# A gated delta rule whose GpSimd and VectorE instructions issue in the order in which they are written

## The chip, the cores and the metric

One core of one Trainium2 chip. The metric is the device time of one execution in microseconds (us), lower is better. A profile of one execution gives the engines' instructions: PE (TensorE), with PEld for its weight loads, DVE (VectorE), ACT (ScalarE), POOL (GpSimd) and SP (SyncE, which here only issues DMAs). L12 is line 12 of the kernel.

## The reference, cut to what matters

A decoder layer over 4 sequences of 512 tokens and 512 channels: a gated delta rule with 16 heads of 128, a cross attention with fake quantisation, and an attention with a mixture of 8 experts. Each of the three takes a layer norm of x, and adds its result to x. Only the first is changed:

```
q = conv_silu(x @ Wq.T)          # causal, four taps; the same for k and v
g = exp(-exp(A_log) * softplus(x @ Wa.T + dt_bias)); beta = sigmoid(x @ Wb.T)
q, k = l2norm(q), l2norm(k)
def step(S, (q_t, k_t, v_t, g_t, beta_t)):
    error = v_t - g_t * (S.T @ k_t)
    S = g_t * S + outer(k_t, beta_t * error)
    return S, S.T @ q_t
o = o * rsqrt(mean(o*o) + eps) * norm_w * silu(x @ Wg.T)
return o @ Wo.T
```

## The kernel before

The delta rule is computed in chunks of 128 tokens, four to a sequence (`TB`). Within a chunk the recurrence is a triangular system: a strictly lower matrix `at`, made of k @ k.T with its decays, has to be inverted as (1 - A). After that a chunk takes a few matmuls with the state.

The work goes by pairs of heads (`HG` = 2): 4 sequences of 8 pairs, 32 pairs (`NP`), numbered m. The work of a pair is cut into Python generators, each of which emits instructions and yields between them:

- `stage1(m)`: key and query projections and convolutions (`conv`: four matmuls L503, one ACT L511, three DVE instructions L514, a Silu L517), transposes of the keys, the norms `ss` and what follows from them on POOL (`rk`, `ee`, `ke`, `nr`, L558 to L562), the decays `em` by a scan on DVE (L567) and scaled on ACT (L397), the matrix `at` (L579), written to DRAM (`at_d`), the scaled query `qg` (L590), `pt` (L601) and the query norms `rq`. `load_blocks` brings the 32x32 blocks of `at` of all chunks into `iA`, one block to a partition, and an identity into `iT`.
- `stage2_inverse(m)`: inverts those blocks by elimination, 31 steps of two instructions (L644, L645), on DVE for even m and on POOL for odd m. It writes `iT` to DRAM (`t_d`, L648), copies its transpose over `iA` (L649), writes that (`x_d`, L650), and loads both back as whole chunks, `T` (L653) and `X` (L655).
- `stage2_values(m)`: value projection, convolution and transposes (`vn`, L674), and the gates `gs`.
- `stage3(m)`: four joins, which make the inverse of 128x128 from the blocks (matmuls L704/L705, L714/L716, L727, L736, with copies from PSUM between them, L707 to L738), then the chunks in turn: `r` (DVE L760), `u` (ACT L769), the state (DVE L782), the output in `po` (PE L785, L787). The gates are multiplied by the query norms on POOL (L745) before the first chunk. At the end `og` (L796) and `cv` (L800) read `po`, a Square on ACT (L802, L804) and a sum on POOL (`acc`, L805) follow.
- `output(m)`: og @ Wo added up in `xa` over the pairs of a sequence (L825, L830); after a sequence's last pair the normalised result is added to x, which is loaded again into `x_in` (L821), and written to `x1d` (L843, L845).
- `prologue(b)` makes the layer norm, its transpose and the gates of a sequence, `prepare` the keys and values of the cross attention.

The main loop runs `stage3(m)` and, after each of its 15 yields, one turn of everything else; what is left is run at the end of the pair. In a turn `stage1` and `stage2_inverse` take two steps, the others one:

```
            if m:
                rest.append((output(m - 1), 1))
            if m + 2 < NP:
                ...
                rest.append((stage1(m + 2), 2))
            if m + 1 < NP:
                rest.append((stage2_values(m + 1), 1))
                rest.append((stage2_inverse(m + 1), 2))
            ...
            rest = turns(*rest)
            for _ in stage3(m):
                next(rest, None)
            run(rest)
```

So the elimination of pair m + 1 is written beside `stage3(m)`, and the matrix that it needs was written beside `stage3(m - 1)`. That is the order of writing. The framework then schedules: it orders each engine's instructions by its own estimate of when each can start, with the written order as priority, and sets semaphores for every dependence. Each engine works through its queue in the order so fixed. A tile with `bufs=n` has n buffers, used in turn; an allocation waits until the readers of the buffer's last contents are done.

Of the kernel before, what the change touches and what calls it, by code (L numbers as in the profile page):

```python
# [98 lines left out]
def decoder(ctx: ExitStack, tc: tile.TileContext, a: dict, out: bass.AP):  # L99
# [69 lines left out]
    def idle(n):  # L169
        for _ in range(n):  # L170
            yield
# [154 lines left out]
    with ExitStack() as st:  # L326
# [74 lines left out]
        def prologue(b):  # L401

            x = []
            for c in range(TB):
                t = w2.tile([P, D], F32, name="x_in", bufs=4)
                nc.sync.dma_start(t, x_t[:, b * TB + c, :])
                x.append(t)
            yield
            yield
            for c, t in enumerate(x):  # L410
                run(layernorm(t.unsqueeze(1), t.unsqueeze(1), small))
                if c == 0:
                    xnT = s2.tile([P, KD, S], F32, name="xnT", bufs=2)
                    seqs[b] = [xnT]
                tp = p_b.tile([P, KD, P], F32, name="pb")
                for kd in range(KD):
                    nc.tensor.transpose(tp[:, kd, :], t[:, kd * P : (kd + 1) * P], ident)
                nc.scalar.copy(xnT[:, :, c * P : (c + 1) * P], tp)
                yield
            pab = p_b.tile([P, TB, 32], F32, name="pb")  # L420
            for c in range(TB):
                for kd in range(KD):
                    nc.tensor.matmul(pab[:, c, :], xnT[:, kd, c * P : (c + 1) * P], wab[:, kd, :], start=kd == 0, stop=kd == KD - 1)
            g_a, lg, beta, gam, ngam, gend, gall = (seq.tile([P, H1, TB], F32, name=n) for n in ("g_a", "lg", "beta", "gam", "ngam", "gend", "gall"))
            nc.scalar.activation(beta, pab[:, :, 16:32].rearrange("p i h -> p h i"), AF.Sigmoid)
            nc.vector.tensor_tensor(g_a, pab[:, :, 0:16].rearrange("p i h -> p h i"), along(dtb, TB), ALU.add)


            y, z, w = (small.tile([P, H1, TB], F32, name=n, bufs=1) for n in ("sp_y", "sp_z", "sp_w"))
            nc.vector.scalar_tensor_tensor(y, g_a, -1.0, g_a, ALU.mult, ALU.min)  # L430
            nc.scalar.activation(y, y, AF.Exp)
            yield
            nc.vector.tensor_scalar(w, y, 2.0, None, ALU.add)
            nc.vector.reciprocal(w, w)
            nc.vector.tensor_tensor(z, y, w, ALU.mult)
            nc.vector.tensor_tensor(w, z, z, ALU.mult)
            nc.vector.tensor_scalar(y, w, 1.0 / 17, None, ALU.mult)
            for n in (15, 13, 11, 9, 7, 5, 3):
                nc.vector.scalar_tensor_tensor(y, y, 1.0 / n, w, ALU.add, ALU.mult)
                if n in (11, 5):  # L440
                    yield
            nc.vector.scalar_tensor_tensor(y, y, 1.0, z, ALU.add, ALU.mult)
            nc.vector.tensor_scalar(y, y, 2.0, None, ALU.mult)
            nc.vector.scalar_tensor_tensor(y, g_a, 0.0, y, ALU.max, ALU.add)
            nc.vector.scalar_tensor_tensor(y, y, -1.0, along(alog, TB), ALU.mult, ALU.mult)

            nc.vector.tensor_scalar(lg, y, -200.0, None, ALU.max)
            yield

            lgf = lg.rearrange("p h i -> p (h i)")  # L450
            pg = p_b.tile([P, 3, H1 * TB], F32, name="pb")
            for n, m in enumerate((C_UP, C_LO, C_ONE)):
                nc.tensor.matmul(pg[:, n, :], tab_a[:, m, :], lgf, start=True, stop=True)
            for n, dst in enumerate((gam, gend, gall)):
                nc.scalar.activation(dst.rearrange("p h i -> p (h i)"), pg[:, n, :], AF.Exp)
            nc.vector.tensor_scalar(ngam, gam, -1.0, None, ALU.mult)
            yield

            nc.vector.tensor_scalar(y, lg, -87.0, None, ALU.max)
            nc.vector.tensor_scalar(z, y, float(np.log2(np.e)), None, ALU.mult)  # L460
            nc.vector.tensor_scalar(z, z, MAGIC, MAGIC, ALU.add, ALU.subtract)
            nc.vector.scalar_tensor_tensor(y, z, -0.693145751953125, y, ALU.mult, ALU.add)
            nc.vector.scalar_tensor_tensor(y, z, -1.42860677e-06, y, ALU.mult, ALU.add)
            yield
            nc.vector.tensor_scalar(w, y, 1.0 / 5040, None, ALU.mult)
            for n in (720, 120, 24, 6, 2, 1):
                nc.vector.scalar_tensor_tensor(w, w, 1.0 / n, y, ALU.add, ALU.mult)
            n2 = small.tile([P, H1, TB], mybir.dt.int32, name="n2", bufs=1)
            nc.vector.tensor_scalar(n2, z, 127.0, None, ALU.add)
            nc.vector.tensor_scalar(n2, n2, 23, None, ALU.logical_shift_left)  # L470
            nc.vector.scalar_tensor_tensor(w, w, 1.0, n2.bitcast(F32), ALU.add, ALU.mult)
            yield

            tp = p_b.tile([H1 * TB, 2, P], F32, name="pb")
            nc.tensor.transpose(tp[:, 0, :], w.rearrange("p h i -> p (h i)"), ident)
            nc.tensor.transpose(tp[:, 1, :], gam.rearrange("p h i -> p (h i)"), ident)
            gr = w2.tile([P, TB * 64], F32, name="Y6").rearrange("p (n t) -> p n t", n=2)[0 : H1 * TB]
            nc.scalar.copy(gr, tp)
            nc.gpsimd.memset(gr[:, 0, 0:1], 0.0)
            for n in range(2):  # L480
                nc.sync.dma_start(g_d[b, n], gr[:, n, :])
            seqs[b] += [beta, gam, ngam, gend, gall]
            yield
# [38 lines left out]
        def stage1(m):  # L522
# [48 lines left out]
            for p in range(HG):  # L571
                scale(em[p], em[p], ee, p)
                pk = p_b.tile([P, TB, P], F32, name="pb")
                for c in range(TB):
                    k_ = kT[p][:, c * P : (c + 1) * P]
                    nc.tensor.matmul(pk[:, c, :], k_, k_, start=True, stop=True)
                at = live.tile([P, TB, P], F32, name="at", bufs=6)
                ats.append(at)
                nc.vector.scalar_tensor_tensor(at, pk, -1.0, em[p], ALU.mult, ALU.mult)  # L579
                nc.sync.dma_start(squares(at_d[m % SLOTS][p * TB : (p + 1) * TB]), at)  # L580
# [5 lines left out]
            for p in range(HG):  # L586
                q = s1.tile([P, S], F32, name="qh")
                yield from conv(b, hg, p, 0, wq, q)
                g = live.tile([P, S], F32, name="qg", bufs=4)
                nc.gpsimd.tensor_tensor(g, q, mb[p], ALU.mult)  # L590
                qg.append(g)
                t = w2.tile([P, S], F32, name="cv", bufs=5)
# [4 lines left out]
                for c in range(TB):  # L597
                    cs = slice(c * P, (c + 1) * P)
                    nc.tensor.matmul(pq[:, c, :], kT[p][:, cs], q[:, cs], start=True, stop=True)
                t = live.tile([P, TB, P], F32, name="pt", bufs=4)  # L600
                nc.vector.tensor_tensor(t, pq, em[p], ALU.mult)  # L601
                pt.append(t)
                yield
# [86 lines left out]
        def stage3(m):  # L690
# [13 lines left out]
                    nc.tensor.matmul(py[lo[p], c, :], ats[p][:, c, 32:64], Ts[p][:, c, 0:32], start=True, stop=True)  # L704
                    nc.tensor.matmul(py[hi[p], c, :], ats[p][:, c, 96:128], Ts[p][:, c, 64:96], start=True, stop=True)  # L705
            for p in range(HG):
                nc.vector.tensor_copy(Yd[p][32:64, :, 0:32], py[lo[p]])  # L707
                nc.scalar.copy(Yd[p][96:128, :, 32:64], py[hi[p]])
            yield
            px = p_b.tile([P, TB, 96], F32, name="pb")  # L710
# [4 lines left out]
                for p in range(HG):  # L715
                    nc.tensor.matmul(px[half[p], c, 0:64], Yd[p][:, c, :], odd(Xs[p][:, c, :]), start=True, stop=True)  # L716
            for p in range(HG):
                nc.vector.tensor_copy(Ts[p][32:64, :, 0:32], px[lo[p], :, 64:96])
                nc.scalar.copy(Xs[p][0:32, :, 32:64], px[lo[p], :, 0:32])
                nc.vector.tensor_copy(Xs[p][64:96, :, 96:128], px[hi[p], :, 32:64])  # L720
            yield

            Y6 = []
# [17 lines left out]
            t = w2.tile([P, HG, S], F32, name="rrow", bufs=1)  # L741
            nc.sync.dma_start(chunks(t), r_d[m % SLOTS].rearrange("c t -> (c t)").partition_broadcast(P))
            rb = [t[:, p, :] for p in range(HG)]
            for p in range(HG):
                nc.gpsimd.tensor_tensor(gs[p], gs[p], rb[p], ALU.mult)  # L745

            st_ = [None] * HG
            po = [p_o.tile([P, TB, P], F32, name=f"po{p}") for p in range(HG)]
            for c in range(TB):
# [34 lines left out]
                for p in range(HG):  # L784
                    nc.tensor.matmul(po[p][:, c, :], us[p], pt[p][:, c, :], start=True, stop=c == 0)  # L785
                    if c > 0:
                        nc.tensor.matmul(po[p][:, c, :], st_[p], qg[p][:, cs], start=False, stop=True)  # L787
                st_ = nst
                yield

            og = []
# [18 lines left out]
        def output(m):  # L810
# [4 lines left out]
            wot = w2.tile([P, HG, D], F32, name="wot", bufs=2)  # L815
            nc.sync.dma_start(wot, a["a_wo"][hg])
            xs = []
            if hg == NHG - 1:
                for c in range(TB):
                    xs.append(w2.tile([P, D], F32, name="x_in", bufs=4))  # L820
                    nc.sync.dma_start(xs[c], x_t[:, b * TB + c, :])  # L821
            for c in range(TB):
                pw = p_b.tile([P, D], F32, name="pb")
                for p in range(HG):
# [7 lines left out]
            if hg == NHG - 1:  # L832
# [6 lines left out]
                rsqrt(rs, pq, small, add=1e-6, mul=1.0 / VD)  # L839
                yield  # L840
                for c in range(TB):
                    xr = xs[c]
                    nc.vector.scalar_tensor_tensor(xr, xa[c], rs[:, c : c + 1], xr, ALU.mult, ALU.add)  # L843

                    (nc.gpsimd if m == NP - 1 else nc.sync).dma_start(x1d[b * TB + c], xr)  # L845
                    yield

        def prepare():

            ctx_ = [w2.tile([P, D], F32, name="og", bufs=2) for _ in range(2)]  # L850
            for kt in range(2):
                nc.sync.dma_start(ctx_[kt], a["ctx"][kt * P : (kt + 1) * P])
            wk = [w2.tile([P, D], F32, name="x_in", bufs=4) for _ in range(KD)]
            for kd in range(KD):
                nc.sync.dma_start(wk[kd], a["b_wkv"][kd * P : (kd + 1) * P, 0:D])
            wv = [w2.tile([P, HG, D], F32, name="wot", bufs=2) for _ in range(2)]
# [31 lines left out]
            for c in range(KD):  # L888
# [14 lines left out]
                yield  # L903
                nc.sync.dma_start(x_val_d[:, :, c * P : (c + 1) * P], t.rearrange("p (k c) -> p k c", k=2))

        NP = B * NHG
        load_weights(0, 1, 0, 2, 3, by=nc.scalar)
        start = prologue(0)
# [11 lines left out]
        for m in range(NP):  # L920
# [13 lines left out]
                wx = top.enter_context(tc.tile_pool(name="b_x", bufs=2, side="right", reuse_waits="tile"))  # L934
                rest.append((cross(0), 2))
            if m:
                rest.append((output(m - 1), 1))
            if m + 2 < NP:
                if (m + 2) % NHG == 0:
                    assert (m + 2) // NHG in seqs  # L940
# [574 lines left out]
```

## Time and profile before

| | |
|---|---|
| time, median of 3 runs | 3922.55 us (3909.57 to 3927.0) |
| the profiled execution | 3921.34 us, its span 3919.6 us |
| granted TensorE clock, mean | 0.941 |
| busy in the span | PE 3487.2 us (89%), DVE 2238.4 (57%), ACT 1522.5 (39%), POOL 1373.3 (35%) |
| delta rule | about 0 to 2200 us |
| elimination, 16 pairs each | DVE 178.4 + 177.4 us, POOL 249.3 + 275.1 us |

The busy times are sums over instructions; a busy PE need not be at its peak, as matmuls overlap. Which wait ends last at a place is read from the list of waits and the timeline.

### The profile page before, as it was taken

What the parts mean: (1) busy time and instruction counts of PE and PEld (TensorE: products, weight loads), DVE (VectorE), ACT (ScalarE), POOL (GpSimd) and SP (SyncE); (2) the same over time, 40 slices, a digit from 0 to 9 for tenths busy, and PEclk for the clock granted to TensorE, in tenths of its full rate; (3) what the DMA queues carried; (4) which work ended last, traced back from release to release, by engine and by line L of the source; (5) the groups of instructions that cost most, each with busy time, mean ns of one, the idle gap of its engine ahead of it and who ended that gap; (6) DMA issues with size and microseconds to landing.
All of it is one profiled execution on the core that took longest, in us unless ns stands there. A gap on an engine that the chain in (4) does not pass through costs nothing. (4 is left out here: it accounts for less than half of the span.)

```text
span 3919.6 us, 48951 instructions
## 1 busy us (share of the span) xinstructions
PE 3487.2 (89%) x16466; PEld 1984.1 (51%) x16466; DVE 2238.4 (57%) x5115; ACT 1522.5 (39%) x4190; POOL 1373.3 (35%) x1941
## 2 busy tenths in 40 slices
PE   5898899898989989898989799998998999897897
PEld 3455555555555555555555445554554555453343
DVE  5576657675766666756765466555665655543111
ACT  3434443334343434334333244443443444433121
POOL 1443554344435552455335222112212211210442
PEclk8899999899999998999999899998999999898898
DMA  5324332433243333343332444445444444445344
GB/s 163 107 77 123 98 103 80 130 101 111 82 119 119 98 100 106 97 119 104 96 98 87 158 145 154 137 132 132 146 127 137 153 146 139 141 152 183 79 82 93
DMA packets 391881, 465.56 MB, mean 119 GB/s; under 512 B 128451, under 2 KB 242115, under 8 KB 391440
## 3 DMA queue, kind: packets, MB, share of 16 engines
q1 hardware_dynamic: 380080, 438.03, 37.1%
q0 software_dynamic: 10112, 21.58, 3.1%
q8 instruction: 132, 2.16, 0.2%
q10 hardware_dynamic: 1440, 2.84, 0.2%
q14 instruction: 117, 0.96, 0.1%
HBM read 401.76 MB, written 64.81 MB: 119 GB/s over the span
## 5 line engine op out<-in xcount | busy, mean ns | idle before, releaser
L503 PE MATMUL pb<-xnT,w 128*128 128x512 f32 x2048 | 954.9, 605 | 0.0
L503 PEld LDWEIGHTS pb<-xnT,w 128*128 128x128 f32 x2048 | 381.9, 195 | 423.7 <-issue 419.7
L514 DVE SCALAR_TENSOR_TENSOR cv<-pb,pp,cv 128x511 f32<-128x511 f32 (+2 forms) x576 | 427.3, 742 | 153.0 <-ACT cv L511 144.2
L1067 PE MATMUL pb<-c_q,hT 128*128 128x512 f32 x768 | 362.9, 609 | 7.9 <-DMA c_q<-in_c_wq_dram 3.6
L644 POOL TENSOR_TENSOR iW<-iA,iT 32x31 f32<-32x31 f32 (+15 forms) x496 | 249.3, 503 | 210.3 <-DMA iA<-at_d 140.5
L825 PE MATMUL pb<-wot,og 128*128 128x512 f32 x512 | 264.9, 642 | 32.8 <-DVE og L796 26.5
L645 POOL TENSOR_TENSOR iT<-iT,iW 32x31 f32<-32x31 f32 (+15 forms) x496 | 275.1, 555 | 39.0
L1173 PE MATMUL pw<-c_o,oT 128*128 128x512 f32 x512 | 244.8, 611 | 21.9 <-DMA c_o<-in_c_wo_dram 15.5
L511 ACT ACTIVATE cv<-pb,pp 128x512 f32<-128x512 f32 x192 | 148.2, 772 | 261.2 <-PE pb L503 260.7
L1067 PEld LDWEIGHTS pb<-c_q,hT 128*128 128x128 f32 x768 | 143.8, 196 | 162.2 <-issue 149.4
L1139 ACT ACTIVATE e<-pb,nm,rq 128x128 f32<-128x128 f32 (+3 forms) x256 | 158.0, 626 | 104.2 <-DVE nm L1137 75.2
L274 POOL TENSOR_SCALAR x_e<-x_e 128x1024 f32<-128x1024 f32 x64 | 68.7, 1073 | 334.0 <-ACT x_e L269 256.6
L644 DVE TENSOR_TENSOR iW<-iA,iT 32x31 f32<-32x31 f32 (+15 forms) x496 | 178.4, 360 | 11.7 <-DMA iA<-at_d 0.2
L645 DVE TENSOR_TENSOR iT<-iT,iW 32x31 f32<-32x31 f32 (+15 forms) x496 | 177.4, 358 | 11.9
L269 ACT ACTIVATE x_e<-pb,nm 128x256 f32<-128x256 f32 x256 | 118.1, 475 | 164.2 <-DVE nm L266 160.7
L1163 PE MATMUL po<-eT,val 128*128 128x512 f32 x320 | 171.6, 630 | 10.0 <-ACT eT L1161 7.7
L1133 PE MATMUL pb<-kT,qT 128*128 128x256 f32 (+3 forms) x576 | 163.5, 410 | 3.6 <-ACT x_e L269 3.6
L558 POOL TENSOR_TENSOR rk<-ss,mhalf 128x8 f32<-128x8 f32 x32 | 53.1, 1659 | 322.0 <-DVE ss L557 321.9
L579 DVE SCALAR_TENSOR_TENSOR at<-pb,em 128x512 f32<-128x512 f32 x64 | 44.3, 692 | 199.9 <-ACT em L397 199.9
L1173 PEld LDWEIGHTS pw<-c_o,oT 128*128 128x128 f32 x512 | 94.4, 194 | 125.5 <-issue 92.1
L1420 PE MATMUL pb<-w_gu,eT 128*128 x312 | 142.7, 601 | 3.8 <-issue 3.8
L825 PEld LDWEIGHTS pb<-wot,og 128*128 128x128 f32 x512 | 89.7, 194 | 110.3 <-issue 53.3
(324 smaller groups left out, 6609.7 us busy)
## 6 DMA issues: line engine op xcount, KB each, us to landing
c_o<-in_c_wo_dram SPq DMA_DIRECT2D x128, 512.0 KB, 4.1
c_q<-in_c_wq_dram SPq DMA_DIRECT2D x128, 512.0 KB, 4.6
w<-in_a_w_dram SPq DMA_DIRECT2D x124, 512.0 KB, 3.7
row<-g_d SPq DMA_DIRECT2D x64, 512.0 KB, 3.8
at_d<-at SPq DMA_DIRECT2D x64, 256.0 KB, 4.2
T<-t_d SPq DMA_DIRECT2D x32, 512.0 KB, 6.1
X<-x_d SPq DMA_DIRECT2D x32, 512.0 KB, 6.1
rrow<-r_d SPq DMA_DIRECT2D x32, 512.0 KB, 4.7
```

Source lines behind the costliest of these rows:

```text
L503: nc.tensor.matmul(pj, wt[:, kd, p * P : (p + 1) * P], xnT[:, kd, :], start=kd == 0, stop=kd == KD - 1)
L511: nc.scalar.activation(ac, pj, AF.Identity, bias=cb[:, m, h : h + 1], scale=cw[:, m, h, 3:4])
L514: nc.vector.scalar_tensor_tensor(ac[:, j:], pj[:, : S - j], cw[:, m, h, 3 - j : 4 - j], ac[:, j:], ALU.mult, ALU.add)
L644: eng.tensor_tensor(u, A[:, i, i + 1 :].unsqueeze(2).to_broadcast([nb, n, w]), T[:, i, :w].unsqueeze(1).to_broadcast([nb, n, w]), ALU.mult)
L645: eng.tensor_tensor(T[:, i + 1 :, :w], T[:, i + 1 :, :w], u, ALU.add)
L825: nc.tensor.matmul(pw, og[p][:, c * P : (c + 1) * P], wot[:, p, :], start=p == 0, stop=p == HG - 1)
L1067: nc.tensor.matmul(pj, hT[:, kd, :], w[:, kd % 2, :], start=kd == 0, stop=kd == KD - 1)
L1133: nc.tensor.matmul(ps[:, m, k * P : (k + w) * P], qT[g][:, n + m, :], kT[:, g, j : j + w, :], start=True, stop=True)
L1139: nc.scalar.activation(e[n + m][:, :nk], ps[:, m, :nk], AF.Exp, bias=nm[:, n + m : n + m + 1], scale=rq, accum_out=es[:, n + m : n + m + 1])
L1163: nc.tensor.matmul(po, val[:, g, :], eT, start=k == 0, stop=k == c)
L1173: nc.tensor.matmul(pw, oT[:, h + m, :], w[:, m, :], start=g == 0 and h + m == 0, stop=g == 3 and h + m == 3)
L1420: nc.tensor.matmul(pg, hT[:, kd, :], w_gu[:, bass.ds(e, 1), kd, :, :], start=kd == 0, stop=kd == KD - 1)
```

## The change

Within the delta rule, `tc.manual_schedule` is entered for POOL and DVE: the instructions of these two engines keep the order in which they are written. PE, ACT and SP are scheduled as before. With it come edits of buffers and places: `at` has four buffers for six, `qg` and `pt` six for four, `x_in` two for four (so the loads of x are made one at a time, and the final sum goes into `xa`), `prepare` takes `qg` and `pt` buffers for a weight; three copies of the joins go from DVE to ACT; the two products of the gates on POOL are written behind the second and third chunk of `stage3`; and `output` begins one turn later.

```diff
@@ prologue: loads of x
-            for c in range(TB):
-                t = w2.tile([P, D], F32, name="x_in", bufs=4)
+            def load(c):
+
+                t = w2.tile([P, D], F32, name="xa", bufs=4) if b == 0 and c > 1 else w2.tile([P, D], F32, name="x_in", bufs=2)
                 nc.sync.dma_start(t, x_t[:, b * TB + c, :])
                 x.append(t)
...
+            for c in range(TB if b == 0 else 2):
+                load(c)
...
+                if b > 0 and c + 2 < TB:
+                    load(c + 2)
@@ stage1
-                at = live.tile([P, TB, P], F32, name="at", bufs=6)
+                at = live.tile([P, TB, P], F32, name="at", bufs=4)
...
-                g = live.tile([P, S], F32, name="qg", bufs=4)
+                g = live.tile([P, S], F32, name="qg", bufs=6)
...
-                t = live.tile([P, TB, P], F32, name="pt", bufs=4)
+                t = live.tile([P, TB, P], F32, name="pt", bufs=6)
@@ stage3
-                nc.vector.tensor_copy(Yd[p][32:64, :, 0:32], py[lo[p]])
+                nc.scalar.copy(Yd[p][32:64, :, 0:32], py[lo[p]])
...
-                nc.vector.tensor_copy(Ts[p][32:64, :, 0:32], px[lo[p], :, 64:96])
+                nc.scalar.copy(Ts[p][32:64, :, 0:32], px[lo[p], :, 64:96])
                 nc.scalar.copy(Xs[p][0:32, :, 32:64], px[lo[p], :, 0:32])
-                nc.vector.tensor_copy(Xs[p][64:96, :, 96:128], px[hi[p], :, 32:64])
+                nc.scalar.copy(Xs[p][64:96, :, 96:128], px[hi[p], :, 32:64])
...
-            for p in range(HG):
-                nc.gpsimd.tensor_tensor(gs[p], gs[p], rb[p], ALU.mult)
...
+                if 0 < c <= HG:
+                    nc.gpsimd.tensor_tensor(gs[c - 1], gs[c - 1], rb[c - 1], ALU.mult)
                 yield
@@ output
+            def load(c):
+                xs.append(w2.tile([P, D], F32, name="x_in", bufs=2))
+                nc.sync.dma_start(xs[c], x_t[:, b * TB + c, :])
+
             if hg == NHG - 1:
-                for c in range(TB):
-                    xs.append(w2.tile([P, D], F32, name="x_in", bufs=4))
-                    nc.sync.dma_start(xs[c], x_t[:, b * TB + c, :])
+                load(0)
+                load(1)
...
-                    xr = xs[c]
-                    nc.vector.scalar_tensor_tensor(xr, xa[c], rs[:, c : c + 1], xr, ALU.mult, ALU.add)
+                    xr = xa[c]
+                    nc.vector.scalar_tensor_tensor(xr, xr, rs[:, c : c + 1], xs[c], ALU.mult, ALU.add)
+                    if c + 2 < TB:
+                        load(c + 2)
@@ prepare
-            wk = [w2.tile([P, D], F32, name="x_in", bufs=4) for _ in range(KD)]
+            wk = [live.tile([P, S], F32, name="qg", bufs=6) for _ in range(2)]
+            wk += [chunks(live.tile([P, TB, P], F32, name="pt", bufs=6)) for _ in range(2)]
@@ main loop
+        st.enter_context(tc.manual_schedule(engines={mybir.EngineType.Pool, mybir.EngineType.DVE}))
         NP = B * NHG
...
             if m:
-                rest.append((output(m - 1), 1))
+                rest.append((chain(idle(1), output(m - 1)), 1))
```

Behind the edits the numbers of lines are six to twelve higher: L704 becomes L712, L727 L735, L769 L775, L796 L804, L825 L837.

More of the change, by code (lines that the diff above doesn't have):

```diff
@@ L403, in prologue @@
             x = []
-            for c in range(TB):
-                t = w2.tile([P, D], F32, name="x_in", bufs=4)
+            def load(c):
+                t = w2.tile([P, D], F32, name="xa", bufs=4) if b == 0 and c > 1 else w2.tile([P, D], F32, name="x_in", bufs=2)
                 nc.sync.dma_start(t, x_t[:, b * TB + c, :])
                 x.append(t)
+            for c in range(TB if b == 0 else 2):
+                load(c)
             yield
             yield
-            for c, t in enumerate(x):
+            for c in range(TB):
+                t = x[c]
                 run(layernorm(t.unsqueeze(1), t.unsqueeze(1), small))
```

## The prediction

> **What bounds the kernel now.** I read the busy table by stretch first, to see which part the edit can touch and which engine fills it. The columns are stretch, length, then busy us and instruction count of PE, PEld, DVE, ACT and POOL, then granted clock and DMA.
>
> ```profile
> 190.00:2078.00 1888.00, 1702.11 (x8886) 1011.48 (x8886) 1238.31 (x2587) 761.03 (x2125) 867.19 (x1299) 0.94 0.35 102
> 2220.00:3650.00 1430.00, 1301.54 (x5635) 713.51 (x5636) 781.90 (x2048) 593.96 (x1638) 287.73 (x392) 0.96 0.47 146
> ```
>
> The delta rule ends near 2200 us; the rest is untouched. In its 30 steady pairs of heads PE works 1702 of 1888 us, 90%. A pair takes 62.8 us (32 starts of L796 `og`, 210.96 to 2158.74), about 56 of it matmul. So PE sets the rate and what counts is what stops PE. The list of waits, cut to the first 2220 us, PE rows:
>
> ```profile
> PE ps L777 <- ACT u L769: 45.0, 13, 6.0
> PE ps L767 <- DVE r L760: 36.8, 41, 1.5
> PE pb L825 <- DVE og L796: 26.5, 27, 1.0
> PE pb L727 <- DVE cv L514: 22.2, 14, 2.3
> PE ps L758 <- DVE state L782: 20.0, 12, 8.7
> ```
>
> Total us, times, longest. Adding up all holes of the PE timeline from the first join (148 us) to the last (2113 us) gives some 196 us, or 6.3 a pair: all that a better order could win. No row names L704, the first matmul of a pair's joins. Its operand is the inverse, and the timelines of POOL, SP and PE show why it never waits:
>
> ```profile
> 944.42 0.24 POOL L645 TENSOR_TENSOR iT<-iT,iW 32x31 f32<-32x31 f32 x1
> 944.70 0.33 SPq L648 DMA_DIRECT2D t_d<-iT  x1
> 948.56 0.37 SPq L653 DMA_DIRECT2D T<-t_d  x1
> 993.58 0.27 PE L475 MATMUL pb<-tab,sp_w 128*64 128x128 f32 x1
> 993.89 0.22 PE L704 MATMUL pb<-T,at 128*32 128x32 f32 x1
> ```
>
> The elimination of this pair ended at 944.66, its T was fetched at 948.56, and the join came 45 us later. Over all pairs but the last T is issued 20 to 46 us ahead of its join: the scheduler starts an elimination as soon as its `iA` is in, half a pair or more early. That slack is what I follow through the change.
>
> **What the Trainium skill says.** "DVE: scalar operands, raw-bit mode, write accounting and state across instructions", Flops that outlive an instruction: the DVE's queue is one in-order queue. The trace agrees: DVE sits 9.36 us ahead of `at` (L579, 955.87 us) and runs nothing behind it. "DMA: Bandwidth & Descriptors", Anatomy of one DMA: about 2.0 us fixed per transfer, whatever its size; here the 128 KB t_d takes 2.3. "TensorE: Matmul & The Clock Gate", The HAM clock gate: after an idle window of about 3.4 us the array runs at half rate until it has been busy for another. The trace agrees: eight L503 matmuls take 3.60 us at 891.64, but 5.02 at 963.14, soon after a hole of 5.71 us.
>
> **The change part by part.** The built order shows what the new guard does. In the kernel before, the 62 elimination instructions of a pair stand on DVE or POOL well ahead; in the changed one they stand as written, four to each of the 15 turns of `stage3`. Two and the `iA` copy are left for the sixteenth turn, which is emitted after `stage3` has ended. On DVE (even pairs) the queue reads twelve elimination instructions, og x2, cv x2, two, iA. On POOL (odd pairs): rq x2, eight, acc x2, two, iA. SP follows with t_d, x_d, T, iT, X. PE's order is nearly that of before: the last `po` of a pair, at once the first join of the next (all 31), and six convolution matmuls only behind it. So a loop closes that was open before: last po, og, end of elimination, t_d, T, join. Its price, durations from the trace:
>
> Even pair. After the last `r` twelve instructions stand ahead of og, 3.2 us, against some 2.8 of PE until po is done: 0.4. Semaphore 0.15, og x2 1.40, cv x2 1.27, last two 0.17 + 0.19, SP's reaction 0.1, t_d 2.3, reaction 0.2, T 6.1 (median of 32):
>
> ```profile
> L653 SPq DMA_DIRECT2D T<-t_d x32: 370/392/2188, 105.1 to 2108.8; - x32
> DMA to landing us min/median/max: 3.9/6.1/7.1
> ```
>
> That is 12.3 us of idle PE. With no delay ahead of og and the 3.9 us landing it is 9.3; with 7.1, 13.3.
>
> Odd pair. acc needs og 1.40, the first cv 0.68 and ACT's Square 0.63, which is po + 2.8. But POOL's queue first has to get through rq: sr copied (L610), issue and 1.8 us landing, 0.24 + 1.67, then eight eliminations at about 0.4. That is sr + 7.5, with po ending near sr + 3, so po + 4.5; I take this. acc x2 2.61, last two 0.54, reaction 0.1, 2.3, 0.2, 6.1: 16.3 us. From 12.0 (acc at 2.8, T 3.9, t_d 2.2) to 18.
>
> At the same place the kernel before loses 1.0 (`og` to L825). There are 15 even boundaries (pairs 2 to 30) and 16 odd: 15 x 11.3 + 16 x 15.3 = **+414 us**; bounds 300 and 460. X lands about 2 us after T and is read behind six matmuls: no more.
>
> Joins' copies (L707, L718, L720): 192 of 0.29 us go from DVE to ACT, which is busy 761 of 1888 us. This takes L727's waits on DVE, 22.2 + 4.3 us: **-26**. It costs ACT 6 x 0.26 = 1.5 us a pair, hidden behind the six matmuls. Five copies in a row on ACT could also show: 0 to +30, I take 0.
>
> gs products to c = 1, 2 and qg, pt at six buffers: rk on POOL no longer stands behind gs (2.5 us), and pt no longer waits for po (94.2 us of DVE). With that em comes earlier and `u` (45.0 us of PE) less late. But em's two scans, 3.1 us, now stand behind ss. I take half: **-22**, from 0 to -45.
>
> Other waits in order: r and state share DVE with four eliminations a turn (1.4 us), and DVE stays below PE (48.8 of 60 us in an even stretch). The rsqrt round trips over POOL (0.55 us) block DVE. **+15**, from -70 (the r, state and kT waits gone) to +60.
>
> Clock: each stall is over 3.4 us, so PE restarts at half rate. One window costs 1.7 us of work, two 3.4; but PE is at half rate 6% of the time already, partly here. **+31** (1.0 a pair), from 0 to +105.
>
> `at` at four buffers costs nothing: the slot's last reader (L727) is done 20 us before it is written. x_in at two buffers makes the loads of x (L406, L821) serial, 3.5 us each beside turns of 4 us; prologues are hidden, the last output is not, and start and tail run in order too: **+10**, from -10 to +30. `idle(1)` moves `output` a turn later; the stall covers it. `prepare` only takes other buffers: 0. SP carries the same number of transfers.
>
> Sum: 414 - 26 - 22 + 15 + 31 + 10 = **+422**. On the profiled execution (span 3919.6, time 3921.3) that is 4343; the median of the runs shown is 1.2 us higher. PE has room to absorb a little more of so large a hole (the other engines are level when it restarts), so I say 4330.
>
> **The rivals.** *The loop is shorter and better absorbed.* T lands near 4 us as the queues are empty at the boundary, acc starts at po + 2.8, and most of the 170 us of PE's other holes close while everybody catches up: 300 - 120 + 10, about 4110. For it: T and X often landed beside rrow and row before. Against: T and X still run together, and the remaining holes come from the chain r, u, state, which no stall shortens.
>
> *Faster.* If T were in SBUF when the last po ends, the edits would be what is left: L727 26, `u` 45, `og` 26, so 3921 - 97 = 3824. It decides at the join: the elimination would have to end 9 to 12 us before the po of the pair ahead. The built order forbids it, since its last two instructions stand behind og or acc, which read that very po.
>
> *Head-of-line blocking on DVE.* It would have to turn each of about 15 turns of an even pair into a wait of half a us and up: 15 x 0.5 x 15 = 110 us more, 4440. Against: DVE has 11 us free in such a pair and 32 in an odd one.
>
> *The guard does nothing*, the scheduler's order being the written one: 3921 less the 26 for the copies, which measures as no change or a little less. The built orders differ from pair to pair, so this is all but excluded.
>
> **How the numbers follow.** Main case 0.78, shorter loop 0.11, blocking 0.07, faster 0.03, guard void 0.01. The main case's bounds (about 4200 to 4440) with part of the second make 4180 to 4440. A measurement tells some 0.5%, 20 us, from no change; the main case, the shorter loop and the blocking are all slower by far more, so slower 0.96, same 0.01, faster 0.03.
>
> **What would show it.** Right: in the waits of PE a row for L712 on the DMA of T, with 31 waits and 350 to 480 us; a pair at 72 to 78 us, odd boundaries longer by some 4 us; the gap from T's issue to its join down to its landing. L735's wait on DVE gone. Wrong: no such row, or PE holes at the joins below 9 us; then the elimination ends earlier than its place in the queue says. If the row is there and the time is not, the holes elsewhere closed.

## The result and the profile after

The changed kernel takes **4403.1 us** (median of 4 runs, 4395.2 to 4408.8); the kernel before, on the same chip, 3918.4 (3909.6 to 3927.0). The ratio is 1.1228, 95% interval 1.1197 to 1.1259: 485 us slower. The profiled execution has a span of 4407.0 us against 3919.6, 487 us more. The forecast was 4330 with a range of 4180 to 4440.

The same first view as before, busy time by stretch, for 30 pairs of the changed kernel. Columns: stretch, length, busy us and count of PE, PEld, DVE, ACT, POOL, granted clock, DMA share, GB/s.

```profile
190.00:2540.00 2350.00, 1725.30 (x8990) 990.45 (x8989) 1221.34 (x2446) 810.74 (x2321) 917.26 (x1352) 0.87 0.30 85
```

PE works 1725 us, as before, but in 2350 us: 73%, where it was 90%. No other engine is busier. So the time is in holes of PE. The stretch from the first join to the last shows it best, as it holds the same matmuls in every version. The rows are the kernel before, the changed kernel without its guard (an experiment below, in which all other edits are kept), and the changed kernel; columns as above:

```profile
148.53:2113.07 1964.54, 1766.42 (x9278) 1049.82 (x9277) 1270.73 (x2650) 787.81 (x2202) 924.41 (x1388) 0.94 0.36 104
148.23:2097.99 1949.76, 1715.84 (x9277) 1012.52 (x9276) 1228.00 (x2472) 827.75 (x2388) 919.17 (x1389) 0.94 0.36 104
163.55:2576.25 2412.70, 1773.62 (x9278) 1019.85 (x9277) 1244.26 (x2485) 833.32 (x2388) 955.95 (x1417) 0.88 0.29 84
```

Length less PE's busy time is the holes: 198 us before, 234 without the guard, 639 in the changed kernel. The joins come every 77.8 us instead of 63.4. Of the 487 us, 448 lie between those joins (441 of holes, 7 of longer matmuls), 15 ahead of the first and 24 behind the last.

The list of PE's waits (total us, times, longest) up to 2750 us, past the end of the delta rule:

```profile
PE pb L712 <- DMA T<-t_d: 440.6, 31, 17.7
PE pb L607 <- ACT qh L525: 97.0, 52, 11.6
PE ps L764 <- DVE state L788: 42.9, 15, 3.0
PE pb L423 <- DVE x_in L137: 42.3, 14, 6.1
PE ps L773 <- DVE r L766: 19.2, 23, 3.3
```

Before, no row named the join. Now it leads the list with 31 waits, one at every boundary between pairs. The rows that led before are gone or small: L735 (then L727) on DVE is absent, `u` is down from 45.0 us to 0.9, `r` from 36.8 to 19.2. Three others have grown: `qh` from 10.9, `state` from 20.0, the prologue's transposes from 9.7.

An even boundary (into pair 18) in the timeline; the pair ahead has its last `po` done at 1571.53. Columns: start, length, engine, line, instruction, and in brackets the idle time before it:

```profile
1571.76 1.39 DVE L804 SCALAR_TENSOR_TENSOR og<-po,pp,gs 128x512 f32<-128x512 f32 x2
1573.08 1.27 DVE L808 TENSOR_TENSOR cv<-po,rrow 128x512 f32<-128x512 f32 x2
1574.37 0.32 SPq L750 DMA_DIRECT2D rrow<-r_d  x1
1574.47 0.18 DVE L653 TENSOR_TENSOR iT<-iT,iW 32x31 f32<-32x31 f32 x1
1574.81 0.35 SPq L656 DMA_DIRECT2D t_d<-iT  x1
1580.18 0.38 SPq L661 DMA_DIRECT2D T<-t_d  x1
1584.21 0.26 PE L712 MATMUL pb<-T,at 128*32 128x32 f32 x1 [12.68 <-DMA T<-t_d]
```

This is the loop: og, cv, the last elimination step behind them, t_d, T, join. It has nearly the predicted length (12.7 against 12.3 us) but not the predicted parts. t_d takes 5.4 us from issue to T's issue, not 2.5, and T then lands in 4.0, not 6.1:

```profile
L661 SPq DMA_DIRECT2D T<-t_d x32: 376/436/558, 123.9 to 2572.0; - x32
DMA to landing us min/median/max: 4.0/4.2/4.9
```

The next boundary, an odd one (into pair 19), POOL's timeline; `po` ends at 1642.3 and the join comes at 1659.5:

```profile
1643.51 0.24 POOL L630 TENSOR_SCALAR rq<-rq 128x8 f32<-128x8 f32 x1
1643.83 1.67 POOL L631 TENSOR_TENSOR rq<-rq,mhalf 128x8 f32<-128x8 f32 x1
...
1649.05 2.60 POOL L813 TENSOR_TENSOR acc<-acc,cv 128x512 f32<-128x512 f32 x2
...
1652.03 0.24 POOL L653 TENSOR_TENSOR iT<-iT,iW 32x31 f32<-32x31 f32 x1
```

rq, eight elimination instructions, acc, the last two: acc starts 6.8 us after `po` here. The stall is 16 to 17.7 us at most odd boundaries (12.3 to 14.1 at five: the first, the last, and those beside which a prologue has been written). In all the 15 even stalls take 190 us and the 16 odd ones 250.

### The profile page after: what moved, and what is told of

It is laid out like the page before. It is cut to its first block, busy times and chain, and to the rows that moved or that the text cites. A ratio compares the mean times of both kernels' runs of the same rounds, so it can differ in the third digit from the quotient of the medians.

```text
span 4407.0 us, 48821 instructions
## 1 busy us (share of the span) xinstructions
PE 3508.8 (80%) x16466; PEld 1962.6 (45%) x16466; DVE 2202.8 (50%) x4923; ACT 1567.3 (36%) x4379; POOL 1387.0 (31%) x1941
## 5 line engine op out<-in xcount | busy, mean ns | idle before, releaser
L511 PE MATMUL pb<-xnT,w 128*128 128x512 f32 x2048 | 1038.6, 645 | 5.5 <-DVE xa L842 4.0
L511 PEld LDWEIGHTS pb<-xnT,w 128*128 128x128 f32 x2048 | 402.7, 210 | 433.1 <-issue 398.3
L522 DVE SCALAR_TENSOR_TENSOR cv<-pb,pp,cv 128x510 f32<-128x510 f32 (+2 forms) x576 | 423.5, 744 | 67.0 <-ACT cv L519 56.3
L842 DVE TENSOR_TENSOR xa<-pb,xa 128x512 f32<-128x512 f32 x112 | 77.1, 689 | 665.9 <-PE pb L837 665.9
L712 PE MATMUL pb<-T,at 128*32 128x32 f32 x512 | 20.6, 242 | 440.6 <-DMA T<-t_d 440.6
L566 POOL TENSOR_TENSOR rk<-ss,mhalf 128x8 f32<-128x8 f32 x32 | 94.8, 2964 | 805.8 <-DVE ss L565 805.8
L653 POOL TENSOR_TENSOR iT<-iT,iW 32x31 f32<-32x31 f32 (+15 forms) x496 | 264.8, 534 | 38.9
L837 PE MATMUL pb<-wot,og 128*128 128x512 f32 x512 | 257.7, 627 | 1.7 <-issue 1.5
L652 POOL TENSOR_TENSOR iW<-iA,iT 32x31 f32<-32x31 f32 (+15 forms) x496 | 238.3, 480 | 38.9
L712 PEld LDWEIGHTS pb<-T,at 128*32 128x32 f32 x512 | 16.4, 152 | 447.1 <-DMA T<-t_d 406.8
L598 POOL TENSOR_TENSOR qg<-qh,row 128x512 f32<-128x512 f32 x64 | 81.9, 1280 | 387.5 <-ACT qh L525 387.5
L653 DVE TENSOR_TENSOR iT<-iT,iW 32x31 f32<-32x31 f32 (+15 forms) x496 | 186.6, 376 | 17.1
L607 PE MATMUL pb<-qh,kT 128*128 128x128 f32 x512 | 93.3, 338 | 97.0 <-ACT qh L525 97.0
```

The source lines that it names most:

```text
L511: nc.tensor.matmul(pj, wt[:, kd, p * P : (p + 1) * P], xnT[:, kd, :], start=kd == 0, stop=kd == KD - 1)
L522: nc.vector.scalar_tensor_tensor(ac[:, j:], pj[:, : S - j], cw[:, m, h, 3 - j : 4 - j], ac[:, j:], ALU.mult, ALU.add)
L566: nc.gpsimd.tensor_tensor(rk, ss, mhalf[:, 0 : HG * TB], ALU.pow)
L652: eng.tensor_tensor(u, A[:, i, i + 1 :].unsqueeze(2).to_broadcast([nb, n, w]), T[:, i, :w].unsqueeze(1).to_broadcast([nb, n, w]), ALU.mult)
L653: eng.tensor_tensor(T[:, i + 1 :, :w], T[:, i + 1 :, :w], u, ALU.add)
L837: nc.tensor.matmul(pw, og[p][:, c * P : (c + 1) * P], wot[:, p, :], start=p == 0, stop=p == HG - 1)
```

## The experiments

Two theories were on trial. **The loop**: what the written order puts ahead of the elimination's last steps, plus the way through DRAM, makes the stall, and the rest of the loss is other in-order waits. **The buffers**: the other edits (four `at`, two `x_in`, copies on ACT) or the busier queues carry a good part of it. Ratios are to the kernel before on the same chip (medians 3926, 3915 and 3915 us in three groups of runs).

**Without the guard.** All other edits kept.

```diff
-        st.enter_context(tc.manual_schedule(engines={mybir.EngineType.Pool, mybir.EngineType.DVE}))
```

> The changed kernel without the written order: both engines are scheduled, all other edits stay (buffers, joins' copies on ScalarE, gate products behind the chunks, output a turn later). Loop theory: no row of L712; waits of L727/L735 on DVE (26 us), of L825/L837 on og (26) and part of those for u (45) gone: 3830 to 3900. Rival (the edits, not the order, made it slow): above 4200.

3921.3 us, ratio 0.999 (0.9981 to 1.0). No wait at L712. The whole loss needs the guard. The expected gain did not come either. L735 waits 4.7 us (26.5 before) and L837 9.8 (26.5 on og before), but `u` waits 77.4 us (45.0 before) and the prologue's transposes 58.3 us behind `xa`: between the joins the holes grow by 36 us. Against that the same matmuls cover 51 us less, 1716 instead of 1766; why they do isn't shown. The edits by themselves are worth next to nothing, but they move time between matmuls and holes, so what the guard costs has to be read against this kernel.

**Three turns of the elimination to a turn of `stage3`.** Written at this rate, its last step is written some four turns before `stage3` ends.

```diff
-                rest.append((stage2_inverse(m + 1), 2))
+                rest.append((stage2_inverse(m + 1), 3))
```

> The changed kernel with one number altered: a turn takes three steps of the elimination, not two, so its 62 instructions, the iA copy and the DMAs are written by the eleventh turn of stage3, four turns ahead of og and acc. Both engines still issue as written. Loop theory (the time went into last po, og or acc, end of elimination, t_d, T, join): T lands some 10 us ahead of the join, the row of L712 on the DMA of T vanishes (440 us), the time is 3950 to 4000, about 4403 - 440, and not quite that of before since PE's waits for qh (97 us) stay. Rival (the written order itself blocks DVE and POOL, whatever stands last): six eliminations a turn block more than four, 4250 or more. Rival (half clock of PE after idle): the time follows the stalls only in part, about 4100.

4008.1 us, ratio 1.0213 (1.0188 to 1.0238), a little above the range. PE's waits:

```profile
PE pb L607 <- ACT qh L525: 92.7, 52, 11.5
PE ps L764 <- DVE state L788: 70.6, 15, 4.7
PE pb L423 <- DVE x_in L137: 46.4, 14, 6.4
PE pb L712 <- DMA T<-t_d: 25.0, 10, 15.0
```

One number in the source takes away 395 of the 485 us, and 416 of the 441 us at L712; of the 25 left, 15 belong to the last pair. T is issued 2 to 10 us ahead of the end of the last `po` at the other boundaries. So the loss at the boundaries is a matter of where the last steps stand. The other three rows stay or grow, but they are no net cost: `u`, the transposes behind `xa`, kT and `r` wait less than without the guard, and apart from L712 the holes between the joins are 241 us against 234. What the profiled execution takes more than the one without the guard, 92 us, is 25 us at L712, 7 in other holes, 36 in matmuls that cover more time (1752 us against 1716), and 24 in start and tail.

**The guard for GpSimd alone, and for VectorE alone.**

```diff
-engines={mybir.EngineType.Pool, mybir.EngineType.DVE}
+engines={mybir.EngineType.Pool}      # first kernel
+engines={mybir.EngineType.DVE}       # second kernel
```

> The changed kernel with the written order for GpSimd alone; VectorE is scheduled again. Loop theory: only odd pairs (eliminated on GpSimd) close the loop, 16 stalls of about 16 us at L712, 250 us, even ones none; the wait for qh goes back to some 10 us as DVE is free again; 3921 + 250 - some 50 for the edits = 4100 to 4160. Rival (VectorE's order is the cost, GpSimd's is harmless): about 3900.

4117.0 us (two runs), ratio 1.0486 (1.0463 to 1.051). As expected: L712 waits 244 us in all, at the 16 odd boundaries only, and at the even ones T is fetched some 40 us ahead. `qh` waits 10.1 us and `state` 6.7, no more than before the change, so the 97.0 and 42.9 us of these two rows need the guard on VectorE. `r` waits 106.3 us.

> The changed kernel with the written order for VectorE alone; GpSimd is scheduled again. Loop theory: only even pairs stall at L712, 15 x 12.7 = 190 us; the wait for qh (97 us) stays; 4080 to 4170. If e2 and e3 add up, (e2 - e4) + (e3 - e4) is the whole distance of the changed kernel from e4. Rival (GpSimd's order is the cost): about 3950.

4390.9 us (two runs), ratio 1.1184 (1.1159 to 1.1209): the expectation missed by 220 us. The two guards don't add up either: over the kernel without a guard they cost 196 and 470 us, 665 together, where both at once cost 482. The stall at an even boundary is not 12.7 but 31 to 32 us (14.3 at the last). SP's queue at one (`po` ends near 1410.7, the elimination is done at 1418.5, the join comes at 1442.4):

```profile
1429.09 0.33 SPq L656 DMA_DIRECT2D t_d<-iT  x1
...
1433.12 0.32 SPq L673 DMA_DIRECT2D r_d<-rq  x1
...
1434.01 0.38 SPq L656 DMA_DIRECT2D t_d<-iT  x1
1438.37 0.38 SPq L661 DMA_DIRECT2D T<-t_d  x1
```

The third row is the store that the join needs. It is ready at 1418.5, but stands behind the t_d of the *next* pair, whose elimination on the unguarded POOL ends only at 1429.07, and behind r_d, which waits for `rq`, which stands behind that same elimination. That wait in the queue is 15.5 of the 31.7 us. The end of the elimination comes later too, 7.8 us after `po` instead of 3.1, as VectorE's steps take 0.6 to 0.7 us beside POOL's (see the last section). With one engine guarded, SP's order, made for the scheduler's estimate, fits neither engine. This is read from one trace; no run takes that order apart.

**Ending the elimination ahead of og and acc.** The last step and the stores are written one turn earlier; the first two steps come in one.

```diff
-                yield
+                if 0 < i < 30:
+                    yield
```

> The changed kernel, but the last elimination step, the transposed copy and the two stores to DRAM are written one turn earlier, ahead of og (VectorE) and acc (GpSimd) of the pair ahead; guard and rate are as in the change. Loop theory (what stands behind og and acc sets the stall): on an even pair the end of the elimination no longer waits for the last po, so its stall falls from 12.7 to 6-8 us; on an odd pair acc leaves the path but rq stays ahead of the last eight steps, so 16.3 falls to 13-14. 16 x 5.5 + 15 x 3 = some 130 us less: 4250-4300, row L712/L713 at 290-340 us. The store of T is then also issued ahead of rrow's 512 KB and lands in 2-3 us instead of 5.4. Rival (the round trip through DRAM, stores and loads behind a busy queue, sets the stall whatever stands in front of it): 4380-4410 with the row still near 430.

4299.3 us, ratio 1.0987 (1.0958 to 1.1017): in the range, at its upper end; the wait at the join (now L713) is 333.9 us. Most odd boundaries fell from 16-17.7 to 12.5-13.9 us, as expected. Even ones fell to 9.1-10.0 (7.5 at the last), not to 6-8, and the timeline of one (pair 16) shows why:

```profile
1370.83 0.18 DVE L653 TENSOR_TENSOR iT<-iT,iW 32x31 f32<-32x31 f32 x1
...
1372.14 0.33 SPq L674 DMA_DIRECT2D r_d<-rq  x1
1372.52 0.42 SPq L502 DMA_DIRECT2D w<-in_a_w_dram  x1
1372.99 0.43 SPq L657 DMA_DIRECT2D t_d<-iT  x1
```

iT is ready at 1371.0, but SP first waits for r_d (that is, for POOL's `rq`) and issues w's 512 KB; then t_d takes 4.2 us, until T's issue at 1377.2. This too is read from the trace; no run takes w's load away.

**The transfer beside t_d.** `rrow` is loaded for the first pair only.

```diff
-            t = w2.tile([P, HG, S], F32, name="rrow", bufs=1)
-            nc.sync.dma_start(chunks(t), r_d[m % SLOTS]...)
+            if m == 0:
+                rows_r.append(w2.tile([P, HG, S], F32, name="rrow", bufs=1))
+                nc.sync.dma_start(chunks(rows_r[0]), r_d[m % SLOTS]...)
+            t = rows_r[0]
```

> The changed kernel with rrow loaded once, for the first pair, and used for all pairs: this leaves out the factor r of the other 31 pairs and takes 31 transfers of 512 KB off SP's queue, that on an even boundary are issued 0.44 us ahead of t_d. If that transfer is what makes the store t_d land in 5.4 us there (1.9 to 2.4 us on odd boundaries), it lands in 2-2.5 us: the even stall falls from 12.7 to 9.5-10, the odd one by 0.3-0.5 (T's load alone in the queue), together 16 x 3 + 15 x 0.4 = 50-60 us, 4340-4360, row L712 at 380-395. Rival: t_d waits 5 us for another reason (w's load, or the small pieces it is written in): row L712 near 430, 4385-4405.

4357.8 us, ratio 1.1127 (1.111 to 1.1143), in the range; the row of the join (now L713) is at 403.3 us, above the 380 to 395 expected. SP's queue at an even boundary:

```profile
1404.88 0.32 SPq L657 DMA_DIRECT2D t_d<-iT  x1
...
1407.37 0.45 SPq L662 DMA_DIRECT2D T<-t_d  x1
```

From t_d to T 2.5 us instead of 5.4; the stall is 10.0 to 10.3 at most of them, instead of 12.7, as expected. So the 3 us were rrow's 512 KB, issued 0.44 us ahead of the 128 KB that the join waits for. At odd boundaries, where rrow goes 4 to 6 us ahead of t_d, nothing changed (250 us in all, as before it), and the 0.4 us expected there are not seen.

**q's third tap a turn earlier**, on top of three turns.

```diff
-                if j == 2:
+                if j == 2 and m:
```

> The changed kernel with three turns of the elimination (4008 us, wait of L607 for qh 93 us) and the third tap of q's convolution written in the turn of the second instead of one turn later. If the 93 us are VectorE's written order, in which the last tap stands behind the elimination steps of a further turn, they fall to 30-50 us and the time to 3950-3970. Rival: the tap only changes place with other VectorE work, and the wait for u, r or state takes over: 3995-4015.

4105.3 us, ratio 1.0483 (1.0462 to 1.0503): some 100 us slower than with three turns alone, and `qh` waits 169.8 us instead of 92.7. Both expectations missed. The edit draws all of q's steps a turn closer together, so the matmuls on `qh` (L607) keep their distance of one turn behind the Silu, while that turn now carries three taps. That explanation is argued, not tested.

**Three turns with the guard on GpSimd alone**, for both parities or for the odd pairs only, and three turns without a guard.

```diff
-engines={mybir.EngineType.Pool, mybir.EngineType.DVE}
+engines={mybir.EngineType.Pool}      # first and second; none in the third
-                rest.append((stage2_inverse(m + 1), 2))
+                rest.append((stage2_inverse(m + 1), 3))     # first and third
+                rest.append((stage2_inverse(m + 1), 3 if m % 2 == 0 else 2))     # second
```

> The changed kernel with the guard on GpSimd alone and three turns of the elimination to a turn of stage3 instead of two. If the 244 us of waits on T of the odd pairs are all that the guard on GpSimd costs beside its gain: 4117 - 244 = about 3870, range 3840-3920, a little faster than before (3926). Rival: the wait for r (106 us with two turns), which comes from eliminations of both engines at one time, grows when GpSimd's is packed closer: r at 150-200 us and 3930-4000, no gain on before.

> As the kernel with the guard on GpSimd alone and three turns, but with three turns only for the eliminations of odd pairs (GpSimd), two for those of even pairs (VectorE, whose instructions the scheduler places anyway). If VectorE's eliminations are placed by the scheduler whatever their turn, the time is that of three turns for both, within 20 us. If the turns bear on where they are placed, the eliminations overlap less and the wait for r is 30-60 us lower than with three turns for both: 20-50 us faster.

> The changed kernel without its guard line, with three turns of the elimination to a turn of stage3. It asks whether the gain of the kernel with the guard on GpSimd alone and three turns (0.992 of before) is the guard's or the turns'. If without a guard the written turn matters little because the scheduler places the elimination anyway: 3905-3930, as without the guard at two turns, and the gain is the guard's. If the gain is the turns': 3870-3895.

3885.5 us, ratio 0.992 (0.9902 to 0.9938); 3886.4, ratio 0.9921 (0.9904 to 0.9938); and 3911.5, ratio 0.9993 (0.9984 to 1.0002). The first:

```profile
PE ps L773 <- DVE r L766: 120.4, 46, 11.5
PE pb L423 <- DVE x_in L137: 24.8, 4, 9.8
PE pb L712 <- DMA T<-t_d: 14.9, 1, 14.9
```

It is the best version, 0.8% faster than before. L712 waits at the last pair only. Of the 244 us of GpSimd's loop 15 are left, the time fell by 5.7% of the kernel before, some 220 us, and `r` grew little. As expected, the turns of the even pairs don't matter where VectorE isn't guarded, and without a guard the turns don't matter at all: the gain needs the guard on GpSimd together with the faster rate. The third kernel, with the same turns and edits and no guard, also says what the guard brings: there `u` waits 76.5 us and the transposes 57.8 behind `xa`, here 4.1 and 24.8, and `r` pays with 120.4 for 29.8. The holes between the joins fall from 230 to 195 us. The edits bring the other part: the matmuls cover 1718 us in the third kernel and 1721 in the first, 1766 before.

## Why the prediction was right, step by step

The range held, and most of the sum is the loop, which the prediction had right. Its sum is 78 us short of the measured 487, and part of the nearness is luck, as the terms show. They are taken from three traces, in us, all but start and tail between the first join and the last. "Edits" is the step from the kernel before to the one without the guard, "guard" the step from there to the changed kernel:

| step | said | before to after | edits | guard |
|---|---|---|---|---|
| loop at the joins, less og's wait | +414 | 440.6 - 26.5 = +414 | -26 | +441 |
| L727's waits | -26 | -25 | -21 | -5 |
| `u` | -22 | -44 | +29 | -73 |
| other in-order waits | +15 | +96 | +54 | +43 |
| half clock (time that the matmuls cover) | +31 | +7 | -51 | +58 |
| start and tail | +10 | +39 | +9 | +30 |
| PE absorbs some | -13 | nothing seen | | |
| sum | +409 | +487 | -6 | +493 |

**The loop** was right in place, count and size (190 us at the even boundaries and 250 at the odd ones, where 185 and 261 were said), and three experiments carry it: without the guard no wait at L712, at three turns 25 us of it, with the last step ahead of og and acc 334. Its parts were not all right. Even: t_d said 2.5 us with its reaction, measured 5.4, because the price came from a place where no large transfer was issued just ahead; T said 6.1, measured 4.0 to 4.9, because the median of before came from a busy queue. The two errors of 2 to 3 us cancel, which is luck. Odd: acc said po + 4.5, measured 6.8 at the boundary shown (POOL is still in earlier elimination steps when `po` ends, so rq starts at po + 1.2), and T again about 1.6 shorter. Two bounds in the working don't add up as written: its short even boundary comes to 9.7 us, not 9.3, its short odd one to 12.4, not 12.0. The sum doesn't use them.

**The other in-order waits** are the term that failed: +15, within -70 to +60, against +96 (`qh` +76, `state` +24, prologue +19, `r` -19, `po` on `u` -10, the rest +6). Prologues were said to be hidden; the transposes, which didn't wait between the joins before, wait 35 us. For `qh` and `state` I had counted that DVE has time left in a pair. What matters is what stands ahead. The timeline inside a pair with the elimination on DVE:

```profile
1545.86 0.40 DVE L652 TENSOR_TENSOR iW<-iA,iT 32x255 f32<-32x255 f32 x1
...
1547.19 0.41 DVE L653 TENSOR_TENSOR iT<-iT,iW 32x256 f32<-32x256 f32 x1
1547.53 0.59 DVE L788 SCALAR_TENSOR_TENSOR state<-state,gall,ps 128x128 f32<-128x128 f32 x2
1547.91 1.05 PE L764 MATMUL ps<-state,kT 128*128 128x128 f32 x4 [2.85 <-DVE state L788]
1548.05 2.95 DVE L522 SCALAR_TENSOR_TENSOR cv<-pb,pp,cv 128x511 f32<-128x511 f32 x4
...
1551.12 2.08 PE L607 MATMUL pb<-qh,kT 128*128 128x128 f32 x8 [2.15 <-ACT qh L525]
```

`state` takes 0.6 us and stands behind four elimination instructions of 1.7 us in all and two taps of 1.5 us; the next taps, 2.95 us, then make `qh` late. So the rival of blocking on DVE, which had 0.07 and 110 us, is seen at work on top of the loop: `qh` and `state` grew by 100 us, though not for its reason alone (half a us in every turn of an even pair), as 33 of the 97 us of `qh` fall beside eliminations on POOL. But it is no net cost. Against the kernel without the guard these two rows grew by 103 us, `u` fell by 73, the prologue by 23, `r` by 14 and kT by 13, and outside the joins the guard leaves 35 us fewer holes.

**The clock** was right in kind and mis-sized, and the +7 hides that. The edits take 51 us off the time that the matmuls cover, for which the sum had no term, and the guard puts 58 on (1.9 a pair), where 31 (1.0 a pair) was said. The clock records of the traces, stretches at full or at half rate, fit: the time covered by matmuls at half rate is 207 us before, 122 without the guard and 247 in the changed kernel, and half of the 125 us between the last two is 62, of the 85 us between the first two 42. Why less half rate falls under the matmuls with the edits isn't shown. Behind each of the 31 joins the half rate lasts 3.4 to 6.1 us, 4.8 in the median, so by an estimate from this a restart costs about 2.4 us of work. Most of the low clock costs nothing: between the joins 598 us are at half rate instead of 236, and 323 of these 363 us fall into holes. The working also has PE at half rate 6% of the time before. It was 236 of 1965 us, 12%: a mean of 0.94 made of stretches at 1 and at 0.5 has 12% of the time at half.

**Start and tail** took 39 us, 30 of them with the guard, where 10 was said and 30 was the bound.

**The rival "faster"** priced the edits at 97 us if T were early. With T early (no guard) they take 6 us off the span, so that price was wrong. The shorter loop was wrong too: T did land near 4 us, but t_d and acc took back what it saved, and PE's other holes grew instead of closing.

## What to carry to other kernels

Before fixing the written order on an engine, look at what stands right ahead of the *last* instruction of each producer: here two of 62 instructions behind a consumer of the previous pair's end closed a loop that cost 11%. Writing the work at a faster rate opened it (4403 to 4008 us); check that against the small, urgent instructions that the faster writing pushes back (`state` waited 70.6 us instead of 42.9). The kernel came out faster than before only where VectorE was left to the scheduler as well (3885 us). A guard on one engine has to be judged with the queues that aren't guarded: SP's order of DMA issues was half of each stall when only VectorE was held to the written order. And a row that grows in a list of waits is no net cost by itself: set the holes and the time under matmuls of both kernels side by side over the same work, and where a change has two parts, against the kernel that has one of them.

## What the hardware showed that was not expected

A 128 KB store issued 0.44 us behind a 512 KB load took 5.4 us until the load that depends on it was issued, and 2.5 without that load ahead.

Behind each of the 31 stalls at the joins, of 10.9 to 17.7 us, PE's clock stayed at half rate for another 3.4 to 6.1 us after the restart.

VectorE and GpSimd slow each other when both eliminate, VectorE far more. VectorE's steps with POOL at the same work (VectorE alone guarded, where POOL runs steps of 32x231 to 32x256 at the time):

```profile
1414.18 0.58 POOL L652 TENSOR_TENSOR iW<-iA,iT 32x240 f32<-32x240 f32 x1
1414.24 0.60 DVE L652 TENSOR_TENSOR iW<-iA,iT 32x60 f32<-32x60 f32 x1
1414.85 0.68 POOL L653 TENSOR_TENSOR iT<-iT,iW 32x240 f32<-32x240 f32 x1
1414.88 0.73 DVE L653 TENSOR_TENSOR iT<-iT,iW 32x60 f32<-32x60 f32 x1
```

In the changed kernel, where the two eliminations run mostly one after the other, the same instructions take 0.21 us each. The Trainium skill, "GPSIMD Engine Reference", section 1, Specifications, says that GpSimd shares its SBUF interfaces with VectorE, with contention for VectorE instructions of two SBUF inputs, which these are; the trace agrees, and the size is its own: about three times at 32x60, twice at 32x207 (0.36 to 0.72 us for L653). Each takes about as long as the GpSimd instruction beside it, 0.58 and 0.68 us here. GpSimd's own steps go up much less, from 0.44 to 0.51 us at 32x156. The kernels with the guard on GpSimd alone lose 106 to 120 us at `r`: in the trace of the one with two turns the scheduler puts VectorE's elimination beside GpSimd's, its steps take 0.5 to 0.7 us, and `r` comes behind them and the taps.
